# A list scheduler's side work: VectorE's stages a step later, finer pieces, late jobs forced alone

## The chip, the cores and the metric

The kernel runs on one core of one Trainium2 chip. The metric is device time in microseconds of one execution, as the median of several; lower is better. A core has TensorE (PE, with its weight loads shown as PEld), VectorE (DVE), ScalarE (ACT), GpSimd (POOL) and SyncE (SP), which issues the DMAs. Each engine works through its own queue in order and waits on semaphores for the others.

## The reference

Eight images of 384 channels and 32 x 32 pixels pass through four layers. Each layer adds a function of the group-normalised input to its input; everything is float32.

```
x = x + mamba(gn(x))                 # layer 0
x = x + fft_gated_conv(gn(x))        # layer 1
x = x + mlp(mamba(layernorm(gn(x)))) # layer 2
x = x + depthwise3x3(gn(x))          # layer 3

def mamba(x):                        # per image, 1024 positions
    xin, z = split(x @ in_proj.T)    # 768 channels each
    u = silu(causal_conv3(xin))
    dt, B, C = split(u @ x_proj.T)
    dt = softplus(dt @ dt_proj.T + b)
    h = exp(dt * A) * h + dt * u * B # 16 states per channel, along the positions
    y = sum_n(h * C) + u * D
    return (y * silu(z)) @ out_proj.T
```

Layer 1 is a 1x1 convolution (`w_in`), a filter on 8 x 8 patches in the frequency domain, a 3 x 3 depthwise convolution, a GELU gate and a 1x1 convolution (`w_out`). The mlp of layer 2 has 1536 hidden channels.

## The kernel before, in words

The work is cut into 32 chunks: 2 mamba layers, 8 images, 2 halves of 512 positions. A chunk has 24 steps (6 blocks of 128 channels, 4 steps each); a step advances 32 channels x 16 states, laid out as 4 tiles of 128 rows x 512 positions. There are 768 steps, and the main loop runs over them. Around the steps, all other work (projections, layers 1 and 3, the mlp) is fitted in as "jobs".

One step t, in the order in which the loop emits it:
- `times(t+1)` (L619): GpSimd multiplies the loaded g (dt·u, spread over the states) by B, in two instructions (L623).
- `scan(t)` (L637): VectorE runs four scans over dA and g (L643), two of which are followed by a multiply with C (L654); GpSimd multiplies the other two tiles by C (L660). `SHARE` says how many tiles VectorE keeps; it is 2 in every entry.
- `jobs.begin`, then `jobs.step(t, 2.0)`: some pieces of other jobs.
- `gather(t-1)` (L664): TensorE sums the 16 states into y; at the end of a block it adds u·D, and VectorE multiplies y by z (L676).
- `begin(t+3)` (L610): SyncE issues the DMA that loads g for three steps later (1 MB). It reads the DRAM tile dud, which a front job must have written.
- `jobs.step(t)`: more pieces.
- `decay(t+1)` (L627): TensorE spreads dt into the four PSUM banks dA, and ScalarE takes Exp in place. These are the same four banks for all steps, so TensorE writes a bank only when the scan (and the multiply) that reads it is done.

Since each engine's queue is in order, where a piece is emitted decides what it runs behind. VectorE's part of a piece emitted in step t runs behind the scans of step t; TensorE's part runs between `decay(t)` and `decay(t+1)`.

A job is a Python generator; each `yield` ends a piece. It has a first step and a due step (`last`), and the jobs are sorted by due step. `Jobs` (L90) keeps a budget per step, `room`, of (TensorE, VectorE) microseconds from `ROOM` (L68); each piece draws it down by what it emits (`mm` at L172 and `Meter` at L71 count columns), and a piece is emitted only if its need, known from an earlier job of the kind, fits. `yield NEXT` lets the job go on only in the next step; `yield EARLY` has its next piece emitted first in the next step; `yield WAIT` says that it cannot go on. `until(done)` (L148) emits pieces of all jobs in due order, without regard to room, until a condition holds: before `begin` needs a dud, and before a scan whose gates are missing.

`pipe` (L189) runs units through stages, each unit with one PSUM bank of a pool of three (`NBANK`, tag `ps`). `live["ps"]` counts the banks in use as of the emission. The pool hands a bank to the next unit as soon as its last reader has been emitted; the wait for that reader is the hardware's, by a semaphore.

The jobs: `front` (L487: load, norm, ps_in with the conv taps on VectorE, ps_x, ps_bc, and six ps_dt, whose softplus is Abs, Exp and Ln on ScalarE, then `plus` on VectorE, `times_u` on GpSimd and `spill` to dud), `gates` (L440: ps_z and Silu), `measure` (L399: statistics), `finish` (L717: `out_proj`, L681, and for layer 2 `mlp`, L891, with ps_up and ps_dn), `layer1` (L796) and `layer3`.

Of the kernel before, what the change touches and what calls it, by code (L numbers as in the profile page):

```python
# [48 lines left out]

SHARE = {"l0_": ((2, 2, 2, 2), (2, 2, 2, 2)), "l2_": ((2, 2, 2, 2), (2, 2, 2, 2))}  # L50
# [17 lines left out]
ROOM = {"l0_": (5.2, 3.0), "turn": (6.4, 3.0), "l2_": (6.4, 3.0)}  # L68
# [21 lines left out]
class Jobs:  # L90
# [3 lines left out]

    def __init__(self, work):
        self.work, self.jobs, self.needs = work, [], {}
        self.room = [0.0, 0.0]

    def add(self, kind, gen, first, last):
        self.jobs.append({"kind": kind, "gen": gen, "first": first, "last": last, "had": [], "got": None})  # L100
# [5 lines left out]
    def piece(self, job):  # L106

        before = list(self.work)
        got = next(job["gen"], self)
        if got is WAIT:  # L110
            return False
        took = tuple(x - y for x, y in zip(self.work, before))
        job["had"].append(took)
        self.room = [x - y for x, y in zip(self.room, took)]
        job["got"] = got
        if got is self:
            self.needs[job["kind"]] = job["had"]
            self.jobs.remove(job)
        return True
# [4 lines left out]
    def begin(self, room):  # L124
        self.room = [max(min(x, y / 8), -y) + y for x, y in zip(self.room, room)]
        early = [job for job in self.in_order() if job["got"] is EARLY]
        for job in self.jobs:
            if job["got"] is NEXT:
                job["got"] = None
        if early:  # L130
            self.piece(early[0])

    def step(self, t, most=None):
# [3 lines left out]
        while went and not (most and self.work[0] >= most):  # L137
            went = False
            for job in self.in_order():
                need = self.need(job)  # L140
                if job["got"] is None and job["first"] <= t and all(
                    y == 0 or x >= y - 0.1 for x, y in zip(self.room, need)
                ):
                    went = self.piece(job)
                    if went:
                        break

    def until(self, done):  # L148

        while not done():  # L150
            if not any(self.piece(job) for job in self.in_order()):
# [4 lines left out]
def tile_conv_preact_d4(ctx: ExitStack, tc: tile.TileContext, a: dict, out: bass.AP):  # L156
# [10 lines left out]
    live = {"ps": 0, "dt": 0, "x": 0, "spm": False}  # L167
# [21 lines left out]
    def pipe(units, deep=2):  # L189
# [3 lines left out]
        units = deque(units)  # L193
        while units or flying:
            went = bool(flying)
            for f in list(flying):
                if f["stages"]:
                    f["stages"].popleft()(f["ps"])
                settle(f)
                if not f["stages"]:  # L200
                    flying.remove(f)
            if units and live["ps"] < NBANK and len(flying) < deep:
# [4 lines left out]
                stages[0](ps)  # L207
                f = {"stages": deque(stages[1:]), "ps": ps, "bank": True}
                settle(f)
                if f["stages"]:  # L210
                    flying.append(f)
            if units or flying:
                yield None if went else WAIT

    def settle(f):
        if f["bank"] and (not f["stages"] or f["stages"][0] is None):
            f["bank"] = False
            ps_done()
            if f["stages"]:
                f["stages"].popleft()  # L220
# [143 lines left out]
    def depthwise(pool, rows, todo):  # L364
# [13 lines left out]
        for q, (n, t) in enumerate(taps):  # L378
            if t == 0:
                ps = yield from ps_tile("ps_dw")  # L380
            _, window, take = todo[n]
# [5 lines left out]
            if t == 8:  # L387
                take(ps[:rows])
                ps_done()
            if t % 3 == 2:  # L390
                yield
# [7 lines left out]
    def measure(s):  # L399
# [12 lines left out]
        live["spm"] = True  # L412
# [7 lines left out]
        def all_read():  # L420
            live["spm"] = False
# [3 lines left out]
    def project(s, d, at):  # L425


        def run(ps):
            for k in range(KC):
                mm(  # L430
                    ps,
                    s["w"]["in"][:, k, at + d * P : at + (d + 1) * P],
                    s["xn"][:, k, :],
                    start=k == 0,
                    stop=k == KC - 1,
                )

        return run

    def gates(s, h):  # L440
# [7 lines left out]
        def evict(d):  # L448
# [3 lines left out]
            ("ps_z", [both(project(s, h * NH + d, DI), evict(d))]) for d in range(NH)  # L452
        )
        yield EARLY
# [5 lines left out]
    def layer_norm(xn):  # L460
        ps = yield from ps_tile("ps_ln")
        for k in range(KC):
            mm(ps, ln_mean, xn[:, k, :], start=k == 0, stop=k == KC - 1)
        for k in range(KC):
# [3 lines left out]
        while live["spm"]:  # L468
            yield WAIT
        ps = yield from ps_tile("ps_lv")  # L470
        for k in range(KC):
            sq = wk.tile([P, T], F32, tag="spm", name="sq", bufs=2)
            act(sq, xn[:, k, :], AF.Square)
            mm(ps, ln_mean, sq, start=k == 0, stop=k == KC - 1)
        rsqrt(ps, ps, eps_ln)
        yield
# [10 lines left out]
    def front(s):  # L487

        c, n = s["c"], s["n"]
        while n > 0 and ("gates", 1) not in chunks[n - 1]:  # L490
# [28 lines left out]
        def taps(d):  # L519
# [10 lines left out]
            ("ps_in", [both(project(s, d, 0), tap(d), taps(d))]) for d in range(ND)  # L530
        )
        if c > 0:
# [18 lines left out]
        for d in range(ND):  # L551
            mm(ps[:RX, :], w["x"][:, d, :], u[d], start=d == 0, stop=d == ND - 1)
        dbc = wk.tile([RX, T], F32, tag="dbc", name="dbc")
        act(dbc, ps[:RX, :], AF.Identity, bias=one_row)
        ps_done()
        yield NEXT
# [9 lines left out]
        def step_dt(d):  # L566
# [10 lines left out]
            def plus(ps):  # L577
                v = s["dt"][d] = wk.tile([P, T], F32, tag="dt", name="dt", bufs=NDT)
                vector.scalar_tensor_tensor(v, ps, 0.0, got["m"], ALU.max, ALU.add)

# [11 lines left out]
            return [both(log, plus), None, both(times_u, spill)]  # L592
# [3 lines left out]
        flying = []  # L596
        for d in range(ND):
            while live["dt"] >= NDT or live["spm"]:
                yield WAIT
            live["dt"] += 1  # L600

            flying.append(pipe([("ps_dt", step_dt(d))]))
            flying = [f for f in flying if next(f, f) is not f]
            yield NEXT
        while flying:
            flying = [f for f in flying if next(f, f) is not f]
            yield NEXT
# [29 lines left out]
    def scan(s, i):  # L637

        g = s["g", i]
        own = SHARE[s["pre"]][s["c"]][i % NSUB]  # L640
        for j in range(4):
            q = 4 * i + j
            nc.vector.tensor_tensor_scan(  # L643
                dAs[j] if j < own else g[:, j, :],
# [6 lines left out]
            if j < own:  # L651
                if s["c"] < NCH - 1:
                    nc.vector.tensor_copy(carry[:, q : q + 1], dAs[j][:, T - 1 : T])
                nc.vector.tensor_mul(g[:, j, :], dAs[j], s["bc"][:, 1, :])  # L654
        if s["c"] < NCH - 1:
            nc.vector.tensor_copy(  # L656
                carry[:, 4 * i + own : 4 * i + 4].unsqueeze(2), g[:, own:4, T - 1 : T]
            )
        g = g[:, own:4, :]
        nc.gpsimd.tensor_mul(  # L660
            g, g, s["bc"][:, 1, :].unsqueeze(1).to_broadcast([P, 4 - own, T])
        )

    def gather(s, i):  # L664
# [8 lines left out]
        if sub == NSUB - 1:  # L673
            u = s["u"][k // NH][:, k % NH, :]
            mm(y, s["w"]["D"][:, k, :], u, start=False)
            nc.vector.tensor_mul(u, y, s["z", k // NH][:, k % NH, :])  # L676
# [4 lines left out]
    def out_proj(s):  # L681
# [14 lines left out]
        def part(m, h):  # L696
            def run(ps):
                for d in range(h * NH, (h + 1) * NH):
                    mm(
                        ps, s["w"]["out"][:, d, m * P : (m + 1) * P],  # L700
                        s["u"][h][:, d % NH, :], start=d == 0, stop=d == ND - 1,
# [4 lines left out]
        def stages(m):  # L706
            if last:
                return [part(m, 0), both(part(m, 1), lambda ps: act(s["t"][m], ps, AF.Copy))]
            return [
                part(m, 0),  # L710
                both(part(m, 1), lambda ps: vector.tensor_add(x[:, m, :], ps, x[:, m, :])),
            ]

        yield from pipe(("ps_out", stages(m)) for m in range(KC))
        s["free"] = True

    def finish(s):  # L717

        yield from out_proj(s)
# [6 lines left out]
        if s["pre"] == "l2_":  # L726
            if s["c"] == NCH - 1:
                jobs.add("layer3", layer3(s), 0, t + 3 * NQ - 1)
        elif s["c"] == NCH - 1:
            until = 2 * NQ + 3 if s["n"] == B * NCH - 1 else 3 * NQ - 2  # L730
            jobs.add("layer1", layer1(s), 0, t + until)
# [33 lines left out]
    def patch_pair(xl, hb, pp):  # L765
# [28 lines left out]
        return pixels, both(frequencies, filtered), back  # L794

    def layer1(s):  # L796
# [3 lines left out]
        for hb in range(H // PS):  # L800

            xl = p1.tile([P, KC, 2, P], F32, tag="xl", name="xl")
            for k in range(KC):
# [7 lines left out]
                )  # L811
            yield NEXT
            for stages in zip(*(patch_pair(xl, hb, pp) for pp in range(2))):
                yield from pipe(("ps_t", [stage]) for stage in stages)
                yield NEXT
        for hf in range(2):
            gate = p1.tile([Q96, 2, 512], F32, tag="acc", name="gate")

            def some(j):
# [9 lines left out]
                return w1dw[:, j, :], window, take  # L829
# [8 lines left out]
            def outward(m):  # L838
# [8 lines left out]
                return [both(run, lambda ps: vector.tensor_add(xc, ps, xc))]  # L847

            yield from pipe(("ps_o1", outward(m)) for m in range(KC))
            yield  # L850
# [40 lines left out]
    def mlp(s):  # L891
# [12 lines left out]
        for half in range(2):  # L904
# [32 lines left out]
            def down(m):  # L937
# [20 lines left out]
                return [sum_up(0, 0), sum_up(0, 1), sum_up(1, 0), both(sum_up(1, 1), add)]  # L958

            yield from pipe([("ps_dn", down(m)) for m in range(KC)], deep=1)  # L960

    def layer3(s):
# [3 lines left out]
        for k in range(KC):  # L966
# [4 lines left out]
            for hf in range(2):  # L971
# [10 lines left out]
                yield from depthwise(p2, P, [(dw3[:, k, :], window, take)])  # L982
# [24 lines left out]
    for t in range(total):  # L1007
# [3 lines left out]
        if i == 0:  # L1011
            jobs.add("gates", gates(s, 1), t + 1, t + 8)
            if s["c"] == 0 and n + NCH < len(chunks):
                jobs.add("measure", measure(chunks[n + NCH]), t, t + NQ + 4)
            if later:
                jobs.add("front%d" % (later["pre"] == "l2_"), front(later), t + 3, t + 14)
                jobs.add("gates", gates(later, 0), t + 13, t + NQ + 2)
        if i == 3 and n == B * NCH:
            load_diagonal(s["w"], s["pre"])
        if i % (NH * NSUB) == NSUB:  # L1020
            jobs.until(lambda: ("gates", i // (NH * NSUB)) in s)
# [5 lines left out]
        if t > 0:  # L1027
            p, q = steps[t - 1]
            gather(p, q)
            if q == NQ - 1:  # L1030
# [142 lines left out]
```

## Time and profile before

| what | value |
|---|---|
| median of 3 runs | 7937.99 us (7935.25 to 7953.73) |
| the profiled execution | 7942.61 us, span 7940.8 us |
| mean granted TensorE clock | 0.919 |
| TensorE busy | 7334.3 us, 92% |
| VectorE busy | 5717.7 us, 72% |
| GpSimd busy | 5639.5 us, 71% |
| ScalarE busy | 4052.0 us, 51% |
| DMA | 1122.90 MB, 141 GB/s over the span |

Busy times are sums over the engine's records. A matmul's end is modelled and may hold waiting time. The steps differ in length: a step's length is read from the start of its first scan to the start of the next step's. In layers 0 and 1 a chunk takes 197 to 232 us, in layers 2 and 3 from 246 to 270 us with a few exceptions around the turn.

### The profile page before, as it was taken

Reading aid. Unit: us, or ns where it says so; the run is one execution under the profiler, and the core shown is the slowest. Engines: PE = TensorE matmul, PEld = TensorE weight load, DVE = VectorE, ACT = ScalarE, POOL = GpSimd, SP = SyncE. Lnnn points to the kernel's source line nnn. Section 1 sums busy time; section 2 is a strip of 40 time slices with the busy share of each in tenths; the row PEclk is TensorE's granted clock in tenths of the full one; section 3 lists DMA queues with packets and bytes.
Section 4 is the critical chain, followed back from the end, with each engine's and each line's share of the span. In section 5 each row is a group of like instructions: output and inputs, shape, how many; then the busy total and the mean of one; then the engine's idle time right before and its main releaser. Section 6 shows DMA issues by size and latency. Waiting matters only on the chain. (4 is left out here: it accounts for less than half of the span.)

```text
span 7940.8 us, 76871 instructions
## 1 busy us (share of the span) xinstructions
PE 7334.3 (92%) x25954; PEld 3037.2 (38%) x25954; DVE 5717.7 (72%) x7254; ACT 4052.0 (51%) x6980; POOL 5639.5 (71%) x2710
## 2 busy tenths in 40 slices
PE   7989999999998999989999989999899989999898
PEld 2223333333333333333334444444444444344445
DVE  5988788878787878778737647767767676676770
ACT  4445545555555555554544545555555555555553
POOL 5888888877787878777737746767767667676770
PEclk8888888989898999989889989999999999999999
DMA  5665655555564656556526645666656666565662
GB/s 138 148 148 137 144 135 136 134 133 137 133 149 118 146 129 143 122 141 151 122 69 173 159 121 144 154 158 165 157 134 163 166 149 159 138 171 140 168 157 65
DMA packets 289704, 1122.90 MB, mean 141 GB/s; under 512 B 37402, under 2 KB 91754, under 8 KB 191004
## 3 DMA queue, kind: packets, MB, share of 16 engines
q1 hardware_dynamic: 289308, 1117.98, 57.2%
q8 instruction: 205, 3.36, 0.2%
q14 instruction: 191, 1.56, 0.1%
HBM read 1042.34 MB, written 75.50 MB: 141 GB/s over the span
## 5 line engine op out<-in xcount | busy, mean ns | idle before, releaser
L623 POOL TENSOR_TENSOR g<-g,bc 128x1024 f32<-128x1024 f32 x1536 | 3586.5, 2357 | 181.3 <-DMA g<-dud 164.4
L660 POOL TENSOR_TENSOR g<-g,bc 128x1024 f32<-128x1024 f32 x768 | 1805.8, 2351 | 1609.5 <-DVE carry L656 871.8
L241 ACT ACTIVATE dA<-dA,w_A 128x512 f32<-128x512 f32 x3072 | 1858.3, 661 | 1480.3 <-PE dA L177 1467.3
L177 PE MATMUL dA<-dt,selr 32*128 32x512 f32 x6144 | 1521.9, 676 | 67.8 <-DVE g L654 59.2
L643 DVE TENSOR_TENSOR_SCAN dA<-dA,carry,g 128x512 f32<-128x512 f32 x768 | 986.7, 1285 | 750.5 <-issue 375.4
L643 DVE TENSOR_TENSOR_SCAN dA<-dA,g 128x512 f32<-128x512 f32 x768 | 940.8, 1225 | 554.3 <-ACT dA L241 221.6
L654 DVE TENSOR_TENSOR g<-dA,bc 128x512 f32<-128x512 f32 x1536 | 1054.5, 687 | 29.8 <-DVE dA L643 0.5
L177 PE MATMUL y<-g,sely 128*32 128x512 f32 x6144 | 934.2, 640 | 47.6 <-POOL g L660 42.4
L643 DVE TENSOR_TENSOR_SCAN g<-dA,carry,g 128x512 f32<-128x512 f32 x768 | 940.4, 1266 | 0.0
L643 DVE TENSOR_TENSOR_SCAN g<-dA,g 128x512 f32<-128x512 f32 x768 | 893.7, 1206 | 0.0
L177 PEld LDWEIGHTS dA<-dt,selr 32*128 32x128 f32 x6144 | 452.1, 192 | 947.2 <-DVE g L643 473.9
L177 PE MATMUL ps_up<-t,mw 128*128 128x256 f32 x2304 | 605.4, 411 | 144.4 <-ACT h L241 100.5
L177 PE MATMUL ps_dn<-h,mw 128*128 128x256 f32 x2304 | 566.1, 397 | 67.7 <-DMA mw<-in_l_mlp_w 55.9
L177 PE MATMUL ps_z<-xf,w_in 128*128 128x512 f32 x1152 | 590.0, 653 | 27.8 <-DVE dt L85 24.0
L177 PE MATMUL ps_dw<-tp,diag 96*96 96x512 f32 x1152 | 580.7, 645 | 14.3 <-ACT diag L241 14.3
L177 PEld LDWEIGHTS ps_up<-t,mw 128*128 128x128 f32 x2304 | 444.9, 201 | 371.0 <-ACT h L241 186.7
L177 PE MATMUL ps_in<-xf,w_in 128*128 128x512 f32 x1152 | 556.2, 623 | 25.3 <-DVE u L85 22.0
L177 PE MATMUL ps_out<-u,w_out 128*128 128x512 f32 x1152 | 548.7, 623 | 9.1 <-DVE x L85 9.1
L177 PEld LDWEIGHTS ps_dn<-h,mw 128*128 128x128 f32 x2304 | 436.7, 196 | 260.3 <-issue 121.0
L177 PE MATMUL ps_dw<-xp,diag 128*128 128x512 f32 x864 | 405.4, 620 | 41.0 <-ACT diag L241 40.9
L241 ACT ACTIVATE h<-ps_up,vec 128x256 f32<-128x256 f32 x384 | 177.3, 474 | 442.7 <-PE ps_up L177 442.4
L241 ACT ACTIVATE u<-ps_in,w_vec 128x512 f32<-128x512 f32 x192 | 149.4, 778 | 478.1 <-PE ps_in L177 478.1
(98 smaller groups left out, 6514.5 us busy)
## 6 DMA issues: line engine op xcount, KB each, us to landing
g<-dud SPq DMA_DIRECT2D x768, 1024.0 KB, 7.1
mw<-in_l_mlp_w SPq DMA_DIRECT2D x384, 384.0 KB, 7.2
dud<-du SPq DMA_DIRECT2D x768, 64.0 KB, 1.7
xk<-in_x SPq DMA_DIRECT2D x48, 256.0 KB, 4.1
xf<-in_x SPq DMA_DIRECT2D x16, 768.0 KB, 8.5
x<-in_x SPq DMA_DIRECT2D x16, 768.0 KB, 8.4
x_mid<-x SPq DMA_DIRECT2D x16, 768.0 KB, 4.7
xk<-x_mid SPq DMA_DIRECT2D x48, 256.0 KB, 5.4
```

What stands on the lines that cost most here:

```text
L177: nc.tensor.matmul(out_, lhsT, rhs, start=start, stop=stop)
L241: nc.scalar.activation(out_, in_, func, **kw)
L623: nc.gpsimd.tensor_mul(g, g, s["bc"][:, 0, :].unsqueeze(1).to_broadcast([P, 2, T]))
L643: nc.vector.tensor_tensor_scan(dAs[j] if j < own else g[:, j, :], dAs[j], g[:, j, :], 0.0 if s["c"] == 0 else carry[:, q : q + 1], ALU.mul ...
L654: nc.vector.tensor_mul(g[:, j, :], dAs[j], s["bc"][:, 1, :])
L660: nc.gpsimd.tensor_mul(g, g, s["bc"][:, 1, :].unsqueeze(1).to_broadcast([P, 4 - own, T]))
```

## The change

All operations stay as they are; what moves is where they stand in the engines' queues.

- In `pipe`, a stage after `NEXT` is emitted in the next step (`f["at"]`); `in_turn` starts no new unit in a call in which another went on. The VectorE stages of ps_in (taps), ps_dt (`plus`), ps_out, ps_dn, ps_o1, the patches' filter and the second half of the depthwise tiles come after a `NEXT`.
- Pieces are finer: `project` in 2 + 1 matmuls, `out_proj` in six parts, the depthwise taps one by one, `mlp`'s ps_dn with two units in flight.
- `until(done, kind)` emits the named kind first, and the check for the gates moves behind `gather`, ahead of the multiply (`gated`).
- A piece is emitted if the room is at least half its need; `ROOM` grants less VectorE time; what may be carried over changes.
- In `layer1`, both patches of a row pass through each stage together, and the next row's `xl` is made early.
- `out_proj` becomes a job of its own; the due steps are new; `SHARE` goes, as 2.

```diff
-ROOM = {"l0_": (5.2, 3.0), "turn": (6.4, 3.0), "l2_": (6.4, 3.0)}
+ROOM = {"l0_": (5.5, 1.8), "turn": (6.6, 1.8), "l2_": (6.6, 1.8)}
...
-        job["got"] = got
+        job["at"] = self.now + (got in (NEXT, EARLY))
+        job["early"] = got is EARLY
...
     def begin(self, room):
-        self.room = [max(min(x, y / 8), -y) + y for x, y in zip(self.room, room)]
...
+        self.now += 1
+        self.room = [max(min(x, 0.8), -y / 2) + y for x, y in zip(self.room, room)]
...
     def step(self, t, most=None):
...
-                if job["got"] is None and job["first"] <= t and all(
-                    y == 0 or x >= y - 0.1 for x, y in zip(self.room, need)
+                if (
+                    job["at"] <= self.now
+                    and not job["early"]
+                    and job["first"] <= t
+                    and all(y == 0 or x >= y / 2 for x, y in zip(self.room, self.need(job)))
                 ):
...
-    def until(self, done):
+    def until(self, done, kind=None):
         while not done():
-            if not any(self.piece(job) for job in self.in_order()):
+            late = [job for job in self.in_order() if job["kind"] == kind]
+            if not any(self.piece(job) for job in late + self.in_order()):
...
-    def pipe(units, deep=2):
+    def pipe(units, deep=2, in_turn=False):
         flying = []
         units = deque(units)
+        def go(f):
+            stages = f["stages"]
+            if stages:
+                stages.popleft()(f["ps"])
+            if f["bank"] and (not stages or stages[0] is None):
+                f["bank"] = False
+                ps_done()
+                if stages:
+                    stages.popleft()
+            if stages and stages[0] is NEXT:
+                stages.popleft()
+                f["at"] = jobs.now + 1
+            if not stages:
+                flying.remove(f)
         while units or flying:
-            went = bool(flying)
+            went = False
             for f in list(flying):
-                if f["stages"]:
-                    f["stages"].popleft()(f["ps"])
-                settle(f)
...
+                if f["at"] <= jobs.now:
+                    went = True
+                    go(f)
-            if units and live["ps"] < NBANK and len(flying) < deep:
+            if (
+                units and live["ps"] < NBANK and len(flying) < deep and not (in_turn and went)
+            ):
...
+            if not went and flying:
+                yield NEXT
+                for f in flying:
+                    f["at"] = 0
...
             if t == 8:
+                if later:
+                    yield NEXT
                 take(ps[:rows])
                 ps_done()
-            if t % 3 == 2:
-                yield
+            yield
...
         yield from pipe(
-            ("ps_in", [both(project(s, d, 0), tap(d), taps(d))]) for d in range(ND)
+            (("ps_in", project(s, d, 0, tap(d)) + [NEXT, taps(d)]) for d in range(ND)),
+            deep=NBANK,
+            in_turn=True,
         )
...
-            return [both(log, plus), None, both(times_u, spill)]
+            return [log, NEXT, both(plus, times_u), None, NEXT, spill]
...
-        return pixels, both(frequencies, filtered), back
+        return [pixels], [frequencies, NEXT, filtered], [back]
...
-                return [sum_up(0, 0), sum_up(0, 1), sum_up(1, 0), both(sum_up(1, 1), add)]
-            yield from pipe([("ps_dn", down(m)) for m in range(KC)], deep=1)
+                return [sum_up(0, 0), sum_up(0, 1), sum_up(1, 0), sum_up(1, 1), NEXT, add]
+            yield from pipe([("ps_dn", down(m)) for m in range(KC)], in_turn=True)
...
         if i == 0:
-            jobs.add("gates", gates(s, 1), t + 1, t + 8)
+            jobs.add("gates1", gates(s, 1), t + 1, t + 1)
...
-                jobs.add("front%d" % (later["pre"] == "l2_"), front(later), t + 3, t + 14)
-                jobs.add("gates", gates(later, 0), t + 13, t + NQ + 2)
+                jobs.add("front%d" % (later["pre"] == "l2_"), front(later), t + 2, t + 5)
+                jobs.add("gates0", gates(later, 0), t + 13, t + NQ - 3)
...
-        if i % (NH * NSUB) == NSUB:
-            jobs.until(lambda: ("gates", i // (NH * NSUB)) in s)
...
             gather(p, q)
+            if q % NSUB == NSUB - 1:
+                jobs.until(lambda: ("gates", h) in p, "gates%d" % h)
+            gated(p, q)
             if q == NQ - 1:
-                end = 10 if p["pre"] == "l0_" else 23 if p["c"] == 0 else 16
-                jobs.add("end%d" % (p["pre"] == "l2_"), finish(p), t + 1, t + end)
+                jobs.add("out%d" % (p["pre"] == "l2_"), out_proj(p), t + 1, t + 3)
         if t + AHEAD < total:
             p, q = steps[t + AHEAD]
-            jobs.until(lambda: p.get("dud", {}).get(QUADS[q][0]))
+            jobs.until(
+                lambda: p.get("dud", {}).get(QUADS[q][0]), "front%d" % (p["pre"] == "l2_")
+            )
             begin(p, q)
```

## The prediction

> **What bounds the kernel now.** I read the page's first part, the stages, the groups, the waits, and then single steps in the timeline.
>
> ```profile
> span 7940.8 us, 76871 instructions
> PE 7334.3 (92%) x25954; PEld 3037.2 (38%) x25954; DVE 5717.7 (72%) x7254; ACT 4052.0 (51%) x6980; POOL 5639.5 (71%) x2710
> ```
>
> PE looks full, but it is not. In the chain of work that ended last, 36 matmul records of 512 columns took 15.73 us, 0.437 us each, while the groups give the same shapes 0.62 us: a record's time holds waiting. Counting every record at its spacing in such unbroken runs (0.43 us for 512 columns, 0.216 for 256, 1.06 for the eight dA records of a step) gives 6018 us of matmul.
>
> The stages, cut at the first scan, at chunks 16 and 18 and at the last scan (columns: stretch, its length, busy time of PE, PEld, DVE, ACT, POOL, clock, DMA share, GB/s):
>
> ```profile
> 92.30:3573.50 3481.20, 3283.45 (x10784) 1136.75 (x10784) 2837.24 (x3565) 1818.11 (x3220) 2814.71 (x1349) 0.89 0.58 138
> 4148.80:7741.00 3592.20, 3286.42 (x12866) 1578.24 (x12864) 2473.18 (x3158) 1854.49 (x3045) 2454.31 (x1174) 0.95 0.61 155
> ```
>
> In both, no engine is full: VectorE has 82% and 69%. From first scan to last, 767 steps took 7650 us, 9.97 each; 92 us lie before, 199 after. For each step I added the row durations that stand between its scans on VectorE and between its dA groups on TensorE. The larger of the two, summed over the steps, is 6454 us. The other 1200 us are waits between engines (columns: who waits, for whom, total us, times, longest):
>
> ```profile
> ACT dA L241 <- PE dA L177: 1467.3, 852, 16.8
> ...
> DVE dA L643 <- ACT dA L241: 346.9, 123, 9.1
> ...
> PE ps_z L177 <- DVE dt L85: 24.0, 6, 4.4
> ...
> PE ps_in L177 <- DVE u L85: 22.0, 27, 3.9
> ```
>
> The ring is: TensorE's dA, ScalarE's Exp, VectorE's scan, and then the next dA into the same four banks. TensorE's queue is in order, so anything ahead of dA that waits delays the next scan. One step of that kind, from the timeline (start, length, what):
>
> ```profile
> 2591.03 1.29 DVE L643 TENSOR_TENSOR_SCAN dA<-dA,carry,g 128x512 f32<-128x512 f32 x1 [0.95 <-issue]
> ...
> 2592.53 1.07 PE L177 MATMUL y<-g,sely 128*32 128x512 f32 x8
> ...
> 2597.26 0.67 DVE L85 SCALAR_TENSOR_TENSOR dt<-ps_dt,spm 128x512 f32<-128x512 f32 x1
> ...
> 2597.98 5.43 PE L177 MATMUL ps_z<-xf,w_in 128*128 128x512 f32 x6 [4.38 <-DVE dt L85]
> 2603.34 1.14 PE L177 MATMUL dA<-dt,selr 32*128 32x512 f32 x8
> ```
>
> ps_z needs the bank that dt reads. dt stands behind this step's scans, so TensorE waits 4.38 us, and then runs six records in 5.43 us, 0.905 each: half speed. The next scan starts at 2605.2: 14.2 us for a step whose busiest engine has 7.7.
>
> [...]
>
> **The change, part by part.** Counts stay: 25,954 matmul records, 7254 on VectorE, 290 table loads and the same DMAs. SHARE was 2 everywhere, so its removal costs nothing; y·z (gated) keeps its place on VectorE, and out_proj's 768 KB load of x (8.4 us to land) is issued no later, under a DMA share of 0.6. All the rest is order, and I counted it in the order in which both kernels' instructions stand.
>
> *VectorE a step behind.* A pipe stage after NEXT is emitted once the next step's scan has been emitted, so on VectorE it runs behind that scan. Its bank is counted free at that moment, and the same step's later pieces take it. TensorE then waits, in that step, for all four scans and the late operation. In the kernel before, 38 steps hold a TensorE instruction that waits for a non-scan VectorE operation of its own step; in the changed kernel 256 do. Price of one: scans 6.0 to 6.5 us, plus 0.65 to 1.4 for the operation (rows u, dt, x at 0.67 to 0.74), plus the TensorE work queued behind the wait, dA included, plus 0.9 for Exp (0.66) and hand-over. This exceeds the busiest engine in 238 steps (before: 34):
> - 131 steps in which TensorE would wait 5 us or more (on average it does 0.4 us before the wait and has 7.8 us behind it): 15.78 against 9.13, so 871 us;
> - 31 with 3 to 5 us: 13.12 against 8.86, so 132 us;
> - 76 with less: 2.3 each, 175 us.
> That is 1178 us; the same sum before is 66. In the 34 steps of before the measured step was never under this sum, and on average 1.9 us over.
>
> *Half speed after the wait.* Six steps of before wait 3 us or more; they took 3.3 us over the sum. The changed kernel has 162. Nothing (if the clock recovers behind scans) to 3.3 each; I take 2.4, 390 us.
>
> *Finer pieces, new ROOM, new due times.* The lumps of before (34 to 105 us of TensorE work in one step, at six places in layer 2) become smaller (largest 66), but steps with over 11 us of TensorE work rise from 12 to 35. The busiest-engine sum goes from 6454 to 6670: +216 us.
>
> *Late work forced alone.* ps_x, dbc, ps_bc, dt, a serial ladder across TensorE and ScalarE, stands in one step in 17 chunks instead of 7. Five such steps of before (one: 28.1 us against 14.0) took 9.2 us over the sum on average, so 10 more are 92 us. Their DMAs (dud, 1.7 us to landing, then g, 7.1) still have three steps; hidden.
>
> *Patch rows.* Steps with ps_t fall from 113 to 68; the work is the same and counted above. du (1.27 us on GpSimd, now behind the step's L660) and the later spill on SP's queue hide in GpSimd's 29% idle; without that cover each du would add its 1.27 us, 244 in all.
>
> *Ordinary waits of the other steps.* Before: 1.45 us in each of 733. Part goes: waits for mlp weights (PE ps_dn and ps_up for DMA mw, 95 us together) where feeding is evener, and part falls into steps that now wait anyway. For 605 steps (529 plus the 76 short ones) I take 1.0: 605 us; ends 0.6 and 1.45, 363 and 877.
>
> *Outside the steps.* Head 92; tail 199 less 20 us of TensorE work that now comes earlier: 180.
>
> Sum: 92 + 6670 + 1178 + 390 + 92 + 605 + 180 = 9207, say 9210. The profiled execution was 7942.6 us for a span of 7940.8, and the median 7938.0, so no correction.
>
> **Rivals.**
> - *The waits cost half* (8450 us, slower): TensorE is stalled elsewhere in those steps anyway, and the clock stays up. 92 + 6670 + 589 + 767 × 1.2 + 180. For it: DVE waits on its own in many long steps. Against: in before every such step paid the full sum.
> - *The evenness wins* (7700 us, faster): the bank is in fact free, so the late VectorE stage never holds TensorE, and the evener feeding takes ordinary waits to 1.0. 92 + 6670 + 767 × 1.0 + 180 = 7709. It decides only if the 238 steps pay less than 1 us each, against 4.95 by the sum: (7940 − 7709) / 238. In the timeline above the bank was not free.
> - *Only the forced ladders count* (7955 us, no change): 767 × 1.2 for ordinary waits, 7862, plus 92.
>
> **How the numbers follow.** Chances: full price 0.74, half price 0.18, faster 0.05, no change 0.02, others 0.01. Full price runs from 8740 (half speed 1 us, ordinary 0.6) to 9630 (3.3 and 1.45). The range takes in that and most of the half-price case: 8400 to 9630. A difference of 0.3% is about what a measurement of this kernel can tell from none. Slower 0.94, same 0.01, faster 0.05.
>
> **What would show it.** Right: waits of PE for DVE dt, u, x and acc of hundreds of us; a mean clock well under 0.92; VectorE's share down near 62%; layer 2's steps longer by more than layer 0's (137 of the 238 steps stand in chunks 17 to 31). Wrong: those waits still under 100 us, which would mean that the banks come free some other way, or a step with such a wait that is under 12 us. The ladder is right if step 21 of a chunk takes some 25 us.

## The result, and the profile after

The changed kernel takes 9625.3 us (9621.5 to 9629.8) against 7938.2 us (7935.3 to 7953.7) before: 1.2121 times as long, 95% interval 1.21 to 1.2142. The profiled execution took 9621.8 us, of which the span is 9619.6, so the sum of the prediction can be held against it directly.

The page's first part, and the line of the granted clock from its second part, of the kernel after:

```profile
span 9619.6 us, 77163 instructions
PE 7846.4 (82%) x25954; PEld 3165.3 (33%) x25954; DVE 5706.2 (59%) x7254; ACT 4054.1 (42%) x6980; POOL 5627.3 (58%) x2710
...
PEclk7778878887888878787898889888888888887989
```

The work is the same: 25,954 matmul records (two for each matmul), and VectorE, ScalarE and GpSimd busy for as long as before within 0.3%. Only TensorE's busy time grew, by 512 us, with no record added. It did the same work at a lower clock (mean 0.840 against 0.919); how much of the 512 us is waiting inside the records is not separated. The clock records of both traces hold full and half clock and nothing between: TensorE stood at half clock for 3083 us, 32% of the span, where before it was 1287 us, 16%.

The stages, cut as before at the first scan, at chunks 16 and 18 and at the last scan (stretch, its length, busy time of PE, PEld, DVE, ACT, POOL, clock, DMA share, GB/s):

```profile
91.60:4322.80 4231.20, 3526.47 (x10901) 1196.69 (x10902) 2829.87 (x3569) 1837.07 (x3272) 2808.72 (x1348) 0.82 0.47 113
4933.40:9438.50 4505.10, 3579.83 (x12910) 1664.41 (x12909) 2477.41 (x3160) 1857.79 (x3065) 2444.79 (x1171) 0.86 0.48 123
```

Layer 0's stage grew by 750 us, layer 2's by 913, and the turn between them by 35 (575.3 to 610.6). In both, every engine lost share: the ring is what takes longer. The waits (who waits, for whom, total us, times, longest) say on what:

```profile
ACT dA L258 <- PE dA L182: 2153.1, 865, 20.7
DVE dA L689 <- ACT dA L258: 1039.1, 186, 16.0
PEld ps_dt L182 <- DVE dt L83: 337.5, 74, 9.4
PE ps_in L182 <- DVE u L83: 335.0, 50, 8.7
PE ps_dt L182 <- DVE dt L83: 259.8, 58, 7.8
...
PE ps_gn L182 <- DVE u L83: 73.9, 8, 10.7
PE ps_dw L182 <- DVE u L83: 61.8, 11, 8.7
```

The chain stands in these rows from the bottom up. TensorE waits for VectorE's late operations. The rows of this form for u, dt, x, acc, tpix and st add up to about 1190 us for PE, where before they had 88. Because of that ScalarE waits for dA (2153 against 1467 us), and VectorE waits for ScalarE (1039 against 347).

One such step of the kernel after, step 593, from the timeline (start, length, what; in brackets the idle time before and its releaser):

```profile
7093.96 1.23 DVE L689 TENSOR_TENSOR_SCAN dA<-dA,g 128x512 f32<-128x512 f32 x1 [3.19 <-issue]
...
7097.83 2.33 DVE L689 TENSOR_TENSOR_SCAN g<-dA,g 128x512 f32<-128x512 f32 x2
...
7100.27 2.97 DVE L83 SCALAR_TENSOR_TENSOR u<-ps_in,w_vec,u 128x511 f32<-128x511 f32 x4
...
7101.85 5.38 PE L182 MATMUL ps_in<-xf,w_in 128*128 128x512 f32 x6 [8.65 <-DVE u L83]
...
7113.49 1.14 PE L182 MATMUL dA<-dt,selr 32*128 32x512 f32 x8
...
7113.60 0.47 ACT L258 ACTIVATE h<-ps_up,vec 128x256 f32<-128x256 f32 x1 [1.65 <-PE ps_up L182]
...
7115.40 1.23 DVE L689 TENSOR_TENSOR_SCAN dA<-dA,g 128x512 f32<-128x512 f32 x1 [12.16 <-ACT dA L258]
```

VectorE needs 6.3 us for the scans before it comes to u, and 1.5 for the first two of the four u operations. TensorE, idle for 8.65 us, starts ps_in 0.1 us after that. Six records take 5.38 us, 0.90 each instead of 0.43; the granted clock in this stretch is 0.52. Then TensorE works off all that stands ahead of dA, which starts 11.6 us after ps_in, though the last scan that reads its banks ended at 7100.16. The next scan comes 1.9 us after dA's first record. VectorE stands idle for 12.16 us. The step takes 21.4 us, while its busiest engine has 9.2 us of work.

### The profile page after: what moved, and what is told of

It reads as the page before. It is cut to its first block, busy times and chain, and to the rows that moved or that the text cites. A ratio compares the mean times of both kernels' runs of the same rounds, so it can differ in the third digit from the quotient of the medians.

```text
span 9619.6 us, 77163 instructions
## 1 busy us (share of the span) xinstructions
PE 7846.4 (82%) x25954; PEld 3165.3 (33%) x25954; DVE 5706.2 (59%) x7254; ACT 4054.1 (42%) x6980; POOL 5627.3 (58%) x2710
## 5 line engine op out<-in xcount | busy, mean ns | idle before, releaser
L670 POOL TENSOR_TENSOR g<-g,bc 128x1024 f32<-128x1024 f32 x1536 | 3578.1, 2351 | 41.9 <-DMA g<-dud 41.9
L182 PE MATMUL y<-g,sely 128*32 128x512 f32 x6144 | 1001.3, 691 | 37.1 <-POOL g L704 22.2
L182 PE MATMUL ps_in<-xf,w_in 128*128 128x512 f32 x1152 | 672.1, 725 | 355.2 <-DVE u L83 335.0
L182 PE MATMUL ps_z<-xf,w_in 128*128 128x512 f32 x1152 | 629.1, 680 | 134.1 <-DVE dt L83 45.9
L182 PE MATMUL ps_dn<-h,mw 128*128 128x256 f32 x2304 | 610.7, 421 | 117.8 <-DVE dt L83 35.6
L182 PEld LDWEIGHTS ps_dn<-h,mw 128*128 128x128 f32 x2304 | 471.7, 210 | 333.8 <-issue 117.7
L182 PE MATMUL ps_dw<-xp,diag 128*128 128x512 f32 x864 | 445.9, 658 | 88.8 <-ACT diag L258 29.4
L182 PE MATMUL ps_dt<-dbc,w_dt 25*128 25x512 f32 x384 | 301.1, 888 | 264.0 <-DVE dt L83 259.8
L182 PEld LDWEIGHTS ps_in<-xf,w_in 128*128 128x128 f32 x1152 | 245.0, 227 | 755.5 <-issue 582.3
```

The source lines that it names most:

```text
L182: nc.tensor.matmul(out_, lhsT, rhs, start=start, stop=stop)
L670: nc.gpsimd.tensor_mul(g, g, s["bc"][:, 0, :].unsqueeze(1).to_broadcast([P, 2, T]))
```

## The experiments

Two theories stood against each other. W: a VectorE stage emitted after the next scan gives its bank away while it is still behind that scan, and the waits of TensorE in that step, over that bank, are the loss. L: the loss is in the forced ladders, in which the front's serial steps stand in one step. What the other parts do alone came next. For each kernel I counted, as in the prediction, the steps in which such a wait sets the length by the order of the instructions ("waiting steps"; 34 before, 238 after), and those in which TensorE would wait 3 us or more (6 before, 162 after). Ratios are to the kernel before.

**Same step.** The changed kernel, with VectorE's stages emitted in the step of their matmuls again:

```diff
-            (("ps_in", project(s, d, 0, tap(d)) + [NEXT, taps(d)]) for d in range(ND)),
+            (("ps_in", project(s, d, 0, lambda ps, d=d: (tap(d)(ps), taps(d)(ps)))) for d in range(ND)),
...
-            return [log, NEXT, both(plus, times_u), None, NEXT, spill]
+            return [both(log, plus), None, both(times_u, spill)]
```

and so for the depthwise tiles, ps_out, the filter, ps_o1 and ps_dn.

> The changed kernel with every VectorE stage of a pipe emitted in the same step as its matmuls again; finer pieces, budget, due steps, forced kinds and patch rows stay. Theory W (waits on VectorE's late stage): in the instruction order 140 steps instead of 238 have such a wait on their longest chain, 41 instead of 162 of 3 us or more; the sum of rows falls from 7848 to 6982 us, and with the over-run per step seen so far (1.46 us for free steps, 1.9 and 3.5 for waiting ones) the time is about 8500 us. Rival L (the late front and the fuller steps cost, not the waits): 10 ladders instead of 17, and the time stays over 9300 us.

Measured: 8530.0 us, ratio 1.0761 (1.0723 to 1.0799). The waits of this kernel:

```profile
DVE dA L687 <- ACT dA L258: 632.1, 178, 10.0
PE ps_in L182 <- DVE u L83: 121.2, 24, 7.7
...
PE ps_dt L182 <- DVE dt L83: 7.4, 2, 6.9
```

Undoing this one part gives back 1095 us, 65% of the loss. ps_dt's wait falls from 259.8 to 7.4 us. But ps_in's is still 121, and 140 waiting steps are left (41 of 3 us or more): something else makes such waits too.

**Bank held.** The stages stay late, but the bank counts as in use for one step more, so that nobody takes it while its reader stands behind a scan. `held` does nothing:

```diff
+    def held(ps):
+        pass
...
-            return [log, NEXT, both(plus, times_u), None, NEXT, spill]
+            return [log, NEXT, both(plus, times_u), NEXT, held, None, spill]
```

and `NEXT, held` after the other late stages.

> The changed kernel, VectorE's stages still a step behind, but the PSUM bank is counted free only one step after such a stage, so that TensorE's next unit takes another bank or comes a step later. Theory W, bank form: the waits of TensorE for VectorE's stages of its own step go from 238 to 56 steps, although the stages stay late; three banks held longer force more work at once (37 steps with 1040 us of matmuls), so the time is about 8600 us, 1000 below the changed kernel. Rival D (the delay of the stages itself, through what is needed from them, costs): 9600 us or more, since everything is later still.

Measured: 8758.0 us, ratio 1.1049 (1.1008 to 1.109), some 160 us longer than expected. The waits of this kernel:

```profile
DVE dA L694 <- ACT dA L261: 385.8, 123, 9.5
PEld ps_dt L182 <- DVE dt L83: 65.2, 42, 4.7
...
PE ps_dt L182 <- DVE dt L83: 22.3, 19, 3.9
```

With VectorE just as late, 867 us come back, and 56 waiting steps are left (11 of 3 us or more). So the early reuse of the bank is most of the price, and lateness by itself is not. It is no cure: pieces that find no bank pile up, and 37 fuller steps hold 1040 us of TensorE's work. And with 56 waiting steps this kernel is 228 us slower than the one with the stages in the same step, which has 140. Late stages with held banks have a price of their own; GpSimd, for one, waits 828 us for VectorE's u and dt here and 155 us there. No run separates what that is worth.

**Late stages alone.** The kernel before with the pipe of the changed kernel and the stages after `NEXT`, nothing else:

> The kernel before, with the changed pipe and its late VectorE stages alone; budget, rules, due steps and pieces as before. Theory W: 158 steps with the wait on their longest chain against 34, 115 of them of 3 us or more; sum of rows 7464 us against 6521; about 9100 us. Rival L: within 2% of 7938 us, since the front is due as before and pieces are as before.

Measured: 9135.0 us, ratio 1.1525 (1.1484 to 1.1565), 158 waiting steps, 115 of them of 3 us or more, which take 3.65 us over their chain. Its waits show the same two rows, `PE ps_in L179 <- DVE u L85: 358.8, 54, 10.6` and `PE ps_dt L179 <- DVE dt L85: 229.8, 44, 7.8`. W holds: this part alone, in the kernel before, costs 71% of the whole loss.

**Forced kind alone.** The kernel before, with `until` emitting the named kind first:

```diff
-    def until(self, done):
+    def until(self, done, kind=None):
...
-            if not any(self.piece(job) for job in self.in_order()):
+            late = [job for job in self.in_order() if job["kind"] == kind]
+            if not any(self.piece(job) for job in late + self.in_order()):
```

> The kernel before, with late work forced alone (the named kind first), nothing else. Sum of rows 6548 us against 6521, 43 waiting steps against 34, 18 steps with the front's ladder against 7. Theory W: about 8040 us, at most 1.5% slower. Rival L (ladders of a forced front are the cost): 11 more ladders at 9 us each are 100 us and more, over 8100 us.

Measured: 8136.2 us, ratio 1.0259 (1.0211 to 1.0306): more than W expects, about what L does. 18 steps hold the ladder instead of 7, at 12.0 us each over the sum of their work instead of 10.5, which is 142 us; another 42 come from a longer tail. L is right about the price of a ladder, and it explains some 200 us, not 1690.

**Finer pieces alone.** The kernel before with `project` in 2 + 1 matmuls, `out_proj` in six parts, the depthwise taps and ps_x one or two at a time:

```diff
-            if t % 3 == 2:
-                yield
+            yield
...
-            ("ps_in", [both(project(s, d, 0), tap(d), taps(d))]) for d in range(ND)
+            ("ps_in", project(s, d, 0, both(tap(d), taps(d)))) for d in range(ND)
```

> The kernel before, with the finer pieces alone (project in 2 + 1 matmuls, out_proj in six parts, one depthwise tap a piece, a pause after every second matmul of ps_x); VectorE's stages stay with their matmuls. Theory W (a TensorE instruction that waits for VectorE's work of its own step prices the step, whichever edit puts it there): 147 steps with such a wait on their longest chain against 34, 57 of 3 us or more; sum of rows 6925 us against 6521; about 8480 us. Rival E (finer pieces even out the steps, and only the late stages cost): 7950 us or less.

Measured: 8658.9 us, ratio 1.0915 (1.0877 to 1.0953). Its waits:

```profile
PE ps_in L177 <- DVE u L85: 236.7, 51, 7.7
...
PE ps_dn L177 <- DVE dt L85: 75.8, 14, 5.5
```

There is no late stage in it, and still 147 waiting steps, 57 of 3 us or more. A second source of the same wait: with smaller pieces the end of one unit and the start of the next fall into one step, and the next one's bank is behind the scan again. This part had looked harmless to me.

**Finer pieces taken out of the changed kernel.** If the two sources added up, this would give back some 700 us.

```diff
-        return [part((0, 1)), part((2,))]
+        return [part((0, 1, 2))]
...
-            yield
+            if t % 3 == 2:
+                yield
```

> The changed kernel without the finer pieces (project whole, out_proj in two parts, three depthwise taps a piece, ps_x in one piece); VectorE's late stages and the rest stay. Theory W: 240 waiting steps, 160 of 3 us or more, as in the changed kernel (238 and 162), sum of rows 7767 against 7848; about 9540 us. If finer pieces cost on their own what they cost in the kernel before (714 us), about 8910 us.

Measured: 9510.2 us, ratio 1.1985 (1.196 to 1.201): 115 us. 240 waiting steps remain, as many as in the changed kernel. Alone the finer pieces cost 714 us, beside late stages 115. My reading is that both spend the same step's slack on the same wait.

**Patch rows alone.** The kernel before, with both patches of a row in each stage and the next row's `xl` made early:

```diff
-            for stages in zip(*(patch_pair(xl, hb, pp) for pp in range(2))):
-                yield from pipe(("ps_t", [stage]) for stage in stages)
-                yield NEXT
+            yield from pipe(("ps_t", of) for of in pixels)
+            yield
+            if hb < H // PS - 1:
+                xl = regroup(hb + 1)
+            yield from pipe(("ps_t", of) for of in spectra)
             yield NEXT
+            yield from pipe(("ps_t", of) for of in back)
+            yield
```

> The kernel before, with layer 1's patch rows in fewer steps alone. Theory W: 27 waiting steps against 34, one front ladder against 7, sum of rows 6433 us against 6521; about 7860 us, 1% faster. Rival N (patch rows are off the path): 7935 us.

Measured: 7729.5 us (7717.9 to 7739.8), ratio 0.9747 (0.9707 to 0.9788), 2.5% faster than the kernel before, more than twice the gain that W expected, and the best of all kernels here. The page's first part:

```profile
span 7716.1 us, 76854 instructions
PE 7169.2 (93%) x25954; PEld 2984.4 (39%) x25954; DVE 5726.9 (74%) x7254; ACT 4046.6 (52%) x6980; POOL 5636.6 (73%) x2710
```

Of the gain, 125 us are in layer 0's stage and 93 in the turn, where one step held a forced lump. The same step, the 21st of chunk 17, in both kernels, first the kernel before (columns as for the stages):

```profile
4002.08:4130.99 128.91, 114.93 (x262) 43.73 (x264) 23.19 (x30) 49.79 (x100) 10.11 (x7) 0.93 0.08 26
```

and then the kernel with this edit alone:

```profile
3875.04:3913.63 38.59, 31.97 (x80) 10.48 (x78) 16.09 (x20) 18.22 (x30) 6.71 (x5) 0.86 0.05 11
```

Before, 262 matmul records, layer 1's ps_dw and ps_o among them, were forced in this step ahead of the front that the next scans needed, while VectorE had 23 us of work in 129. Here layer 1 ends in time, and 80 are left. Steps with a ladder fall from 7 to 1, waiting steps from 34 to 27, and the steps that wait for nothing of their own take 1.28 us over their work, not 1.45. About half of that last fall is the six ladders again, as ladder steps are counted among these. How much each of the three adds to layer 0's 125 us is not separated. In the changed kernel this gain lies under the waits.

**Half the need alone.** A piece is emitted when half its need is there (`x >= y / 2` for `x >= y - 0.1`).

> The kernel before, with one line of the change alone: a piece is emitted if the room is at least half its need, instead of need less 0.1 us. Sum of rows 6511 us against 6521, 35 waiting steps, one ladder against 7, and 23 us less TensorE work behind the last step. Theory W: about 7910 us, within 0.5% of before. Rival O (overdrawn steps cost what they overdraw): over 8000 us.

Measured: 7859.3 us, ratio 0.9904 (0.9869 to 0.994): 1.0% faster, where I had expected next to nothing. The gain is in layer 0 (3482 to 3393 us) and the turn (575 to 520); layer 2 loses 87.

**Patch rows with more room**, TensorE's budget at 6.8 in the turn and in layer 2, and **patch rows with half the need**, to see whether the two gains add:

> The kernel before, with the patch rows in fewer steps, and in layer 2 a TensorE room of 6.8 us a step instead of 6.4. Sum of rows 6424 us, 42 waiting steps, none of 3 us or more, 15 us less TensorE work behind the last step: about 7840 us, faster than both kernels. Rival N: 7935 us.

> The kernel before, with the two parts of the change that were faster alone together: patch rows in fewer steps, and a piece emitted at half its need. Sum of rows 6496 us (patch rows alone 6433, half need alone 6511), 44 waiting steps, no front ladder, 23 us less behind the last step. If the gains add up: 7729 less 80, about 7650 us. If the sum of rows decides: about 7770 us, no better than patch rows alone.

Measured: 7772.4 us, ratio 0.9793 (0.9758 to 0.9829), no better than the patch rows alone; and 7907.1 us, ratio 0.9958 (0.9946 to 0.9971). The second was a miss: together the two edits keep only 33 of 215 and 86 us. The steps that wait for nothing of their own are back at 1.55 us over their work, and VectorE's wait for Exp is at 628.7 us (336.8 with the patch rows alone). The granted clock goes the same way: 0.936 with the patch rows alone, 0.916 with both edits. Whether the waits lower the clock or the clock lengthens the waits, no run here separates, and why the two edits disturb each other stays open.

**Keeping TensorE busy in the wait.** The changed kernel, with six matmuls of zero weights at the start of 102 waiting steps, added to the y bank that is open, so that they add zero to it:

```diff
+        if t in WARM:
+            p, q = steps[t - 1]
+            for _ in range(6):
+                nc.tensor.matmul(
+                    p["y", QUADS[q][0]][0:64, :], zeros, _flat(selr), start=False, stop=False
+                )
```

> The changed kernel, and at the start of 102 of the steps in which TensorE would wait 5 us or more, six matmuls of 512 columns with zero weights into the open y bank, which add zero (5.2 us at full clock, so they lie inside the wait). Order and waits of all other work stay. Theory C (the part of these steps beyond the sum of rows is mostly the half clock after the wait): the over-run of 3.6 us falls to the ordinary 1.5, so about 200 us less than 9625, and the mean clock rises from 0.84. Rival: the over-run has another cause, and the time stays at 9625 or rises by what the added matmuls overshoot, up to 100 us.

Measured: 9482.3 us, ratio 1.1946 (1.1925 to 1.1966): 143 us less with 1224 more matmul records. Step 591 after the same wait, first in the changed kernel, from the timeline:

```profile
7070.24 0.47 DVE L83 SCALAR_TENSOR_TENSOR x<-ps_dn,vec,x 128x256 f32<-128x256 f32 x1
7070.43 2.90 PE L182 MATMUL ps_up<-t,mw 128*128 128x256 f32 x6 [6.79 <-issue]
7073.25 1.94 PE L182 MATMUL y<-g,sely 128*32 128x512 f32 x8
```

and then with the zero matmuls:

```profile
6970.33 0.47 DVE L93 SCALAR_TENSOR_TENSOR x<-ps_dn,vec,x 128x256 f32<-128x256 f32 x1
6970.52 1.53 PE L192 MATMUL ps_up<-t,mw 128*128 128x256 f32 x6 [1.50 <-issue]
6971.98 1.06 PE L192 MATMUL y<-g,sely 128*32 128x512 f32 x8
```

The wait ends at the same place, but what follows runs at full speed: six records of ps_up take 1.53 for 2.90 us, eight of y 1.06 for 1.94. The step takes 18.5 us for 21.3. Over the 102 steps it is 1.28 us each (19.39 to 18.11), 130 us in all, less than the 200 expected.

The clock records say why it is not more. Take the stretch from the end of the VectorE operation that TensorE waits for to the end of the step's dA. In the 102 steps of the changed kernel, 5.7 us of it are at half clock on average. With the zero matmuls it is still 2.8, and the steps fall into two kinds. This is that stretch in steps 591 and 552 of the changed kernel (columns as for the stages; the clock stands third from the end):

```profile
7070.33:7083.02 12.69, 12.03 (x47) 7.24 (x47) 0.39 (x1) 2.37 (x5) 5.67 (x3) 0.77 0.52 129
6553.70:6566.73 13.03, 12.97 (x45) 6.82 (x45) 1.08 (x3) 1.86 (x3) 7.75 (x4) 0.73 0.37 84
```

and with the zero matmuls:

```profile
6970.41:6980.33 9.92, 9.25 (x47) 6.00 (x47) 0.40 (x2) 2.37 (x5) 5.69 (x3) 1.00 0.60 149
6461.13:6473.99 12.86, 12.80 (x45) 6.65 (x45) 1.08 (x3) 1.86 (x3) 7.74 (x4) 0.74 0.36 82
```

In 44 steps, like 591, no half clock is left in the stretch: they go from 18.79 to 16.43 us, and what they take beyond their chain falls from about 3.2 to 0.9 us. In the other 58, like 552, the stretch keeps 4.9 of its 6.0 us at half clock, and they gain 0.45 us. There the zero matmuls end on average 3.0 us before the wait does, in the 44 steps 2.0; whether this decides is not shown. So where the clock stayed up, theory C holds: the half clock is the larger part of what a long wait costs beyond its chain, and this run removed only half of it.

## Why the prediction was right, and where its sum was off

The time, 9625 us, lies within the range, and the case forecast as likeliest is the one that came. It lies 415 us above the sum of 9210, though, and 5 us below the upper end: the loss is 1687 us and not the 1270 of the sum, so that the range held it is in part luck. The same accounting on the trace after (head, steps, tail: 92 + 9347 + 181):

| term | predicted us | measured us |
|---|---|---|
| head | 92 | 92 |
| busiest-engine sum | 6670 | 6670, the same order |
| wait chains in 238 steps | 1178 | 1178 by the order; no step of the 162 long ones was under it |
| "half speed" in the 162 steps | 390 (2.4 each) | 578 (3.57 each) |
| ladders | 92, for ten new ones | about 180, for all 17, nearly all inside the next row |
| ordinary waits, 605 steps | 605 (1.0 each) | 920: 776 (1.47 in 529), 144 (1.90 in 76) |
| tail | 180 | 181 |

- **The term furthest off is "ordinary waits".** I let them fall from 1.45 to 1.0 us, since feeding is evener and other steps now wait anyway. The row measures 920 us instead of 605, 1.52 a step. Waits for mlp weights did go (95 us before, 2 after). But the row also holds nearly all ladder steps. Taken with the ladders, 697 us were forecast, and 223 us are missing. With the ladder steps left out on both sides, a step had about 1.35 us of ordinary waits before and has about 1.25 after: they fell, by a quarter of what I had put.
- **The ladders came as forecast.** The 17 steps take 10.8 us over the sum (predicted 9.2), 29.1 on average, and step 21 takes 20 to 32 us in 17 of the 31 chunks measured.
- **"Half speed after the wait" was the right mechanism, and taken too small.** The excess is 3.57 us a step instead of 2.4, 188 us more, and above the upper end of 3.3. That the class begins at a wait of 3 us was an estimate, from six steps of before; no run tests that bound. The clock records put 5.7 us at half clock behind a long wait, on average; as records take about twice as long there (0.90 for 0.43 us), I estimate from this that some 2.8 of the 3.57 us are the half clock. The rest, some 0.7 us, is close to the 0.9 that the 44 steps without half clock keep. My sum had put ordinary hand-overs at nothing in these 162 steps. Step 593 shows two: 0.56 us of TensorE's wait for ScalarE's h between its ps_up groups, and Exp behind another h for 0.47.
- **The chain's price was right, its owner only in part.** Of the 131 steps with a wait of 5 us or more none took under 13.3 us; on average 19.39 against a chain of 15.78. But I gave all 238 steps to the late stages. With them undone 140 are left, and the finer pieces alone make 147. The term of finer pieces was taken at +216 us, of their lumps; alone they cost 714, nearly all through waits and what follows them.
- **"Patch rows: the work is the same"** holds for the sum of work, and missed what the early end of layer 1 does for the lumps: 215 us of gain alone.
- **The signs named beforehand.** PE's waits for VectorE are about 1190 us, hundreds as said. The clock is 0.840. VectorE's share is 59% and not 62%, which is the longer span and nothing else. Layer 2's steps lengthened by 913 us and layer 0's by 750.
- **The rivals.** "The waits cost half" falls: the 162 long steps paid the full chain, each of them. "The evenness wins" would have needed less than 1 us in such a step. "Only the forced ladders count" is worth about 200 us by the run on the forced kind, in the kernel before. GpSimd's du and the spill stayed hidden: dud lands later (median 4.3 us from its issue against 1.7), and GpSimd's wait for the loaded g is 41.9 us over the whole execution, against 164.4 before.

The parts alone, to within some 10 us: late stages +1200, finer pieces +714, forced kind +201, half the need −86, patch rows −215. Without the late stages they nearly add up (+614 against +595 in the run with the stages in the same step). With them they add to 1814, against 1687. The new `ROOM` and what may be carried over, the due steps, `out_proj` as a job of its own and the later check for the gates were not run alone; the near agreement takes them to cancel, which is not shown.

## What to carry to other kernels

In a ring of in-order queues, ask of each operation that frees a buffer what stands ahead of it on its own engine, and who takes that buffer before the ring closes: here an operation that costs 0.7 us on VectorE held TensorE up for as much as 10.6 us (u, in the run with the late stages alone), since it stood behind four scans while TensorE's next piece already had its bank. Count these same-step waits in the order of the instructions before and after an edit; that count foretold most of the differences here, where busy shares did not. It is not the whole price: the kernel with the banks held has fewer such steps than the one with the stages in the same step, and is slower. Then ask of each long wait what clock the work behind it gets (here 0.90 us a record in step 593, instead of 0.43). And run the parts of a bundle alone: one edit of this one is a gain of 2.5%, hidden under three that lose.

## What the runs showed of the hardware that I had not expected

- Work that computes nothing can pay. 1224 matmul records of zero weights shortened the execution by 143 us, 1.5%, with the mean clock at 0.879 for 0.840. In these 102 steps of the changed kernel 5.7 us behind the long wait are at half clock, on average; with the zero matmuls 2.8.
- The same filler work kept the clock up behind the wait in 44 of 102 steps only. In these it ended 2.0 us before the wait did, on average, in the other 58 it was 3.0 us.
- A smaller piece isn't a safer one. Splitting three matmuls into two and one, and its like, with no operation added, cost 9% alone.
- Two edits that gain 2.5% and 1.0% alone gain 0.4% together. I can't say why.
